# Reordering a decoder layer on one core: what stands in which half of a step, smaller pieces, and what is queued first

## The chip, the core and the metric

The kernel runs on one core of a Trainium2 chip. Its time is the time that the device takes for one execution, in microseconds; three runs are given with their median, and one more execution was profiled.

## The reference

One pre-norm decoder layer over 64 sequences of 128 tokens of width 128, with 16 heads of 8, in float32: self-attention, cross-attention to 77 context rows, and a mixture of 8 experts of which each token uses two. Cut to what matters:

```python
def _layernorm(x):                       # no weights
    return (x - mean(x)) / sqrt(var(x) + 1e-5)

def attn(x):                             # 64 x 128 x 128, heads of 8
    q, k, v = heads(x @ Wq.T / sqrt(128)), heads(x @ Wk.T), heads(x @ Wv.T)
    return (softmax(q @ k.T) @ v) @ Wff.T + bff

def xattn(x, ctx, mask):                 # ctx 64 x 77 x 128
    q, k, v = heads(x @ Wq.T + bq), heads(ctx @ Wk.T + bk), heads(ctx @ Wv.T + bv)
    s = where(mask == 0, -1e9, q @ k.T / sqrt(8))
    return (softmax(s) @ v) @ Wo.T + bo

def ffn(x):                              # 8 experts, 128 -> 512 -> 128, top 2 of a cosine gate
    g = l2norm(x @ Wp.T) @ l2norm(sim).T / temperature
    w, which = top_k(g, 2); w = softmax(w)
    return sum(w_e * (gelu(x @ W1[e] + b1[e]) @ W2[e] + b2[e]) for e in which)

x = x + attn(layernorm(x))
x = x + xattn(layernorm(x), ctx, mask)
x = x + ffn(layernorm(x))
```

## The kernel before, in words

**Groups and steps.** Four batches make a group (`GB = 4`), so there are 16 groups; each goes through a self job and a cross job, 32 jobs in all (self jobs first). `x` stays in SBUF in the tiles `xs`. The main loop of `attention` runs over steps `s`, one batch a step: in step `s` it makes the first scores of batch `a = s` (`ps`, 128x512, for the row maxima `m`), the second, transposed scores of batch `t = s - 4` (`pt`, with the maximum folded in by an extra row of `qh`), their exponentials `e`, and the product with the values (`po`) of batch `z = s - 5`. A step has two halves; each makes the scores of two of the four head groups (`score_tiles`), so a block of 16 matmuls (and in cross jobs 4 more for the mask's `bias`). There are three buffers for `ps` and two for `pt`.

**What else stands in a step.** For each job, `prologue` returns a list: normalise the group (`norm`, tile `xn`, on ScalarE), transpose it (`trans`, PE's `tp`), project the queries (`query`, `pq`), keys (`key`, `pk`) and values (`value`, `pv`). Queries and keys are copied to SBUF, written to DRAM (`d`, issued from ScalarE's queue) and read back by SP's queue with the heads spread over partitions (`qh`, `kh`, four loads each); this layout change is why each goes through DRAM. `turn` transposes the row maxima of two batches (`pm`), and sends them by way of DRAM (`md`) into a row of `qh`. `project` applies the output projection (`py`), adds it to `xs` and takes the new statistics. All these are closures in one list, `todo`; each half takes one from it after its block of scores (`next_`), and one more a step when over four wait. `turn` and `project` are put at its front. `soon` holds the division by the softmax sums and the transpose back, `late` the routing of a finished cross group (`route`), at the offsets of `LATER` in halves: normalise, transpose (`tp`), project (`pp`), pick the two largest (`largest`), `count` (with a chain on GpSimd, `ahead`), `place` (`pr`), and then scatters of the rows to their experts' places in DRAM, one a half (`sending`).

**Order on the engines.** The order of PE, VectorE (DVE) and ScalarE (ACT) is as the program is written (`manual_schedule`). GpSimd's (POOL) and SP's instructions are placed by a scheduler, which may put an instruction ahead of earlier ones when it is ready sooner; `issue_after` ties an instruction behind another in its queue.

**Experts.** The groups are in two parts, 11 and 5 groups. When all groups of a part are placed, `table` computes on VectorE which 256-row tile belongs to which expert, and where each row will lie. `experts` then goes through the tiles of a part: fetch rows (`xr`) and copy the expert's weights (`wr`), transpose (`tp`, `xT`), first layer (`ph`) with Gelu, second layer (`py`), store (`yr`). Between tiles of part 0 the rest of the attention's lists is worked off (`more`), between tiles of part 1 the results of part 0 are gathered and added (`some`); at the end those of part 1. Weights of all experts sit in SBUF (`we_s`), loaded by `load_experts`; `spare` writes blocks of zeros behind the rows.

**Start.** `clean(n)` fills the three sets of `kh`, `qh` and `vm` buffers with constants; then come the statistics of group 0, `root(0)` (a chain of eight GpSimd operations for the inverse deviation), the first prologue, the rest of the weights, statistics of groups 1 and 2.

Of the kernel before, what the change touches and what calls it, by code (L numbers as in the profile page):

```python
# [8 lines left out]
F32 = mybir.dt.float32  # L9
# [6 lines left out]
P = 128  # L16
# [9 lines left out]
LATER = (2, 3, 4, 5, 7, 8, 9, 10)  # L26
# [4 lines left out]
def decoder_layer(  # L31
# [43 lines left out]
    for g in range(1, 4):  # L75
        load_x(g)
# [32 lines left out]
    def load_experts():  # L109
        for e in range(E):  # L110
            nc.sync.dma_start(we_s[:, e, 0:F], w1[e])
            nc.sync.dma_start(
                we_s[:, e, F:WF].rearrange("p (c d) -> p c d", d=D),
                w2[e].rearrange("(c f) d -> f c d", f=P),
            )
        nc.sync.dma_start(
            we_s[:, :, WF : WF + NFC], b1.rearrange("p (e c) -> p e c", e=E)
        )
        for e in range(E):
            nc.sync.dma_start(we_s[:, e, WF + NFC :], b2[e].partition_broadcast(P))  # L120
# [44 lines left out]
    def inverse_root(r, v):  # L165

        t = work.tile([P, GB], F32, tag="newton", name="newton")[: v.shape[0], : v.shape[1]]
        nc.gpsimd.tensor_tensor(r, v, half_s[: v.shape[0], : v.shape[1]], ALU.pow)
        nc.gpsimd.tensor_tensor(t, r, r, ALU.mult)
        nc.gpsimd.tensor_tensor(t, t, v, ALU.mult)  # L170
        nc.gpsimd.tensor_scalar(t, t, -0.5, 1.5, ALU.mult, ALU.add)
        nc.gpsimd.tensor_tensor(r, r, t, ALU.mult)

    def root(g):
# [6 lines left out]
        nc.gpsimd.tensor_scalar(shift[:, at], shift[:, at], -1.0, None, ALU.mult)  # L181

    def normalised(g, tag="xn", bufs=1):
        xn = work.tile([P, GB, D], F32, tag=tag, name=tag, bufs=bufs)
        for b in range(GB):
            i = g * GB + b
            nc.scalar.activation(  # L187
                xn[:, b, :], xs[g][:, b, :], AF.Identity,
                bias=shift[:, i : i + 1], scale=rstd[:, i : i + 1],
            )  # L190
        return xn
# [74 lines left out]
    def route(g):  # L266
# [11 lines left out]
        def norm():  # L278
            v["xn"] = normalised(g, "x3", 3)
# [101 lines left out]
        def scatter(b, k, behind):  # L381
# [9 lines left out]
        return [  # L391
            norm, trans, lambda: project(0), lambda: project(1), lambda: largest(0),
# [3 lines left out]
    def table(part):  # L396

        pn = ps_m.tile([P, E], F32, tag="mm", name="pn")
        nc.tensor.matmul(pn, ones_f, part.seen, start=True, stop=True)
        M = part.rows // TILE  # L400
        N = part.tiles
        over = hp.tile([P, E, M], F32, tag="over", name="over", bufs=1)
        need = hp.tile([P, M], F32, tag="need", name="need", bufs=1)
        nc.vector.tensor_scalar(need, tid[:, :M], float(TILE), None, ALU.mult)
        count = hp.tile([P, E], F32, tag="count", name="count", bufs=1)
        nc.vector.tensor_copy(count, pn)
        nc.vector.tensor_tensor(
            over, count.unsqueeze(2).to_broadcast([P, E, M]),
            need.unsqueeze(1).to_broadcast([P, E, M]), ALU.is_gt,
        )  # L410
        nt = hp.tile([P, E], F32, tag="nt", name="nt", bufs=1)
        nc.vector.tensor_reduce(nt, over, AX.X, ALU.add)
        acc = hp.tile([P, E, E], F32, tag="acc", name="acc", bufs=1)
        nc.vector.tensor_tensor(
            acc, low, nt.unsqueeze(1).to_broadcast([P, E, E]), ALU.mult
        )
        end = hp.tile([P, E], F32, tag="end", name="end", bufs=1)
        nc.vector.tensor_reduce(end, acc, AX.X, ALU.add)
        past = hp.tile([1, N, E], F32, tag="past", name="past", bufs=1)
        nc.vector.tensor_tensor(  # L420
            past, tid[:1, :N].unsqueeze(2).to_broadcast([1, N, E]),
            end[:1].unsqueeze(1).to_broadcast([1, N, E]), ALU.is_ge,
        )
        ex = hp.tile([1, N], F32, tag="ex", name="ex", bufs=1)
        nc.vector.tensor_reduce(ex, past, AX.X, ALU.add)
        nc.vector.tensor_tensor(
            past, past, nt[:1].unsqueeze(1).to_broadcast([1, N, E]), ALU.mult
        )
        be = hp.tile([1, N], F32, tag="be", name="be", bufs=1)
        nc.vector.tensor_reduce(be, past, AX.X, ALU.add)  # L430
        nc.vector.tensor_tensor(be, tid[:1, :N], be, ALU.subtract)
        nc.vector.tensor_scalar(be, be, float(TILE), None, ALU.mult)
        rw = hp.tile([1, N], F32, tag="rw", name="rw", bufs=1)
        nc.vector.tensor_scalar(rw, ex, float(part.step), None, ALU.mult)
        nc.vector.tensor_tensor(rw, rw, be, ALU.add)
        part.row = hp.tile([1, N], I32, tag=f"prow{part.n}", name="prow", bufs=1)
        nc.vector.tensor_copy(part.row, rw)
        nc.vector.tensor_scalar(ex, ex, float(E - 1), float(WE), ALU.min, ALU.mult)
        part.wat = hp.tile([1, N], I32, tag=f"pwat{part.n}", name="pwat", bufs=1)
        nc.vector.tensor_copy(part.wat, ex)  # L440

        nc.vector.tensor_tensor(count, count, part.base, ALU.add)
        tail = hp.tile([1, E], I32, tag=f"tail{part.n}", name="tail", bufs=1)
        nc.vector.tensor_copy(tail, count[:1])
        def tail_zeros(e):
            with behind("SP"):
                r = nc.sync.value_load(
                    tail[0:1, e : e + 1], min_val=e * part.step,
                    max_val=e * part.step + part.rows,
                )  # L450
            i = nc.sync.dma_start(
                part.x[bass.ds(r, TILE), :].rearrange("(h p) d -> p h d", p=P), zero_s
            )
            last["SP"] = i.ins
            apart(i.ins, f"x{part.n}")
            part.scatters.append(i.ins)

        clearing.extend(lambda e=e: tail_zeros(e) for e in range(E))
# [5 lines left out]
        less = hp.tile([P, E], F32, tag="less", name="less", bufs=1)  # L464
        nc.vector.tensor_scalar(
            less, nt, -float(TILE), float(part.step), ALU.mult, ALU.add
        )
        sf = slot_f[:, every, :].rearrange("p b k -> p (b k)")
        off = hp.tile([P, 2 * GB * SPLIT], F32, tag="off", name="off")[:, : 2 * GB * K]
        one = hp.tile([P, 2 * GB * SPLIT], F32, tag="one", name="one")[:, : 2 * GB * K]  # L470
        nc.vector.tensor_copy(off, sf)
        for e in range(1, E):
            nc.vector.tensor_scalar(  # L473
                one, sf, float(e * part.step), less[:, e - 1 : e], ALU.is_ge, ALU.mult
            )
            nc.vector.tensor_tensor(off, off, one, ALU.subtract)  # L476
        nc.vector.tensor_copy(back[:, every, :].rearrange("p b k -> p (b k)"), off)
# [19 lines left out]
    def attention():  # L497
        jobs = [(cross, g) for cross in (False, True) for g in range(NGRP)]
        NB = len(jobs) * GB
        with (  # L500
# [27 lines left out]
            nc.vector.tensor_reduce(one, last, AX.X, ALU.add)  # L528
# [523 lines left out]
```

## Time and profile before

| | us |
|---|---|
| runs | 1321.33, 1324.6, 1330.93 (median 1324.6) |
| profiled execution | 1318.96 |
| its span, from the first to the last instruction | 1317.2 |
| PE busy | 1108.3 (84%) |
| VectorE busy | 738.7 (56%) |
| ScalarE busy | 593.8 (45%) |
| GpSimd busy | 491.8 (37%) |
| first block of scores starts | 41.33 |
| last `po` of the attention | 880.76 |
| first `ph` of the expert tiles | 899.3 |
| first `ph` of part 1 | 1104.8 |
| mean granted clock of PE | 0.919 |

Times in the profile count from the first instruction. A line of the waits names who waited for whom, the total in us, how often, and the longest. A line of a table by stretches gives the stretch and its length, then for PE, weight loads (PEld), VectorE, ScalarE and GpSimd the busy time with the number of instructions, then PE's granted clock (1.00 is full), the share of the DMA engines' time, and GB/s. A line of the timeline has start and duration, engine (a "q" behind it: the sequencer, for instance a DMA issue), source line, operation, what it writes and reads, shapes, how many follow each other, and in brackets the idle time before it and who ended it. An instruction count of PE's float32 matmuls is twice that of the program.

### The profile page before, as it was taken

The page shows a single profiled execution, that of the slowest core. Times are in us where ns is not written, and L with a number is a line of the kernel's source. Part 1 is how long each engine was busy: PE and PEld are TensorE (multiplying, and loading weights), DVE is VectorE, ACT ScalarE, POOL GpSimd, SP SyncE. Part 2 cuts the span into 40 slices and gives each one's busy share as a digit, 9 for nine tenths or more (in the row PEclk, how much of TensorE's full clock was granted, in tenths as well). Part 3 has the DMA queues.
Part 4 walks back from the last instruction along what each step waited for, and adds up shares of the span by engine and source line. Part 5 has one row for each costly group of instructions (what it writes and reads, how often), then busy time and mean ns, then how long its engine had stood idle before and what let it go on. Part 6 is the DMA issues. An engine that isn't in the chain of part 4 may idle for free. (4 is left out here: it accounts for less than half of the span.)

```text
span 1317.2 us, 39334 instructions
## 1 busy us (share of the span) xinstructions
PE 1108.3 (84%) x15925; PEld 901.9 (68%) x15925; DVE 738.7 (56%) x2129; ACT 593.8 (45%) x1374; POOL 491.8 (37%) x897
## 2 busy tenths in 40 slices
PE   2799898998999999999999997977989998666920
PEld 1577676777777777777777776756979998555910
DVE  3367676777776545666666667644454444444322
ACT  1145554555555565555655554544434443222400
POOL 5023213323121124555565554462120003777056
PEclk9589898999898999999999998997989999888965
DMA  9623121222121222232222222111223222434222
GB/s 261 147 68 75 37 54 33 56 52 55 38 66 40 51 55 55 62 71 63 67 67 65 68 65 68 34 47 57 74 75 98 73 72 83 114 108 113 59 62 78
DMA packets 120181, 94.99 MB, mean 72 GB/s; under 512 B 22712, under 2 KB 102592, under 8 KB 120000
## 3 DMA queue, kind: packets, MB, share of 16 engines
q1 hardware_dynamic: 97328, 58.73, 18.9%
q0 software_dynamic: 8192, 16.79, 4.5%
q10 hardware_dynamic: 14480, 16.96, 4.0%
q8 instruction: 125, 2.05, 0.7%
q14 instruction: 56, 0.46, 0.2%
HBM read 49.53 MB, written 42.89 MB: 70 GB/s over the span
## 5 line engine op out<-in xcount | busy, mean ns | idle before, releaser
L696 ACT ACTIVATE e<-pt 128x512 f32<-128x512 f32 (+1 forms) x512 | 276.4, 590 | 307.5 <-PE pt L659 148.9
L669 DVE TENSOR_REDUCE m<-ps 128x4 f32<-128x512 f32 (+1 forms) x512 | 274.0, 576 | 218.1 <-PE ps L659 103.1
L650 PE MATMUL ps<-kh,qh 31*128 31x128 f32 (+1 forms) x4096 | 340.7, 295 | 37.0 <-DMA kh<-d 26.0
L650 PEld LDWEIGHTS ps<-kh,qh 31*128 31x128 f32 x4096 | 284.9, 196 | 93.6 <-issue 43.4
L650 PE MATMUL pt<-qh,kh 32*128 32x128 f32 (+1 forms) x4096 | 344.2, 288 | 3.1 <-ACT e L696 1.5
L650 PEld LDWEIGHTS pt<-qh,kh 32*128 32x128 f32 (+1 forms) x4096 | 273.6, 170 | 14.7 <-ACT e L696 4.3
L883 ACT ACTIVATE hT<-ph,wr 128x256 f32<-128x256 f32 x312 | 128.9, 470 | 213.6 <-issue 186.8
L876 PE MATMUL ph<-xT,wr 128*128 128x256 f32 x624 | 163.2, 408 | 50.3 <-DVE xT L868 50.3
L382 POOL DMA_INDIRECT xr<-x,slot x128 | 129.1, 1009 | 192.0 <-ACT e L696 95.9
L929 POOL DMA_INDIRECT r<-yr,back x128 | 124.7, 974 | 191.5 <-DMA yr<-yr 152.7
L876 PEld LDWEIGHTS ph<-xT,wr 128*128 128x128 f32 x624 | 121.2, 205 | 69.6 <-DVE xT L868 54.5
L894 PEld LDWEIGHTS py<-wr,hT 128*128 128x128 f32 x1248 | 154.8, 195 | 4.6
L894 PE MATMUL py<-wr,hT 128*128 128x128 f32 x1248 | 154.4, 278 | 0.0
L711 PE MATMUL po<-e,vm 128*32 128x128 f32 (+1 forms) x4096 | 147.6, 288 | 0.0
L711 PEld LDWEIGHTS po<-e,vm 128*32 128x32 f32 (+1 forms) x4096 | 110.5, 114 | 37.2 <-issue 27.8
L177 POOL TENSOR_SCALAR var<-stat 128x4 f32<-128x4 f32 x48 | 12.0, 250 | 253.9 <-DVE stat L163 243.9
L900 DVE TENSOR_TENSOR yr<-py,wr 128x256 f32<-128x256 f32 x78 | 33.0, 423 | 119.5 <-PE py L894 119.5
L940 DVE SCALAR_TENSOR_TENSOR xs<-r,prob,xs 128x128 f32<-128x128 f32 x128 | 44.6, 351 | 92.3 <-DMA r<-yr,back 91.7
L659 PE MATMUL pt<-ident_b,bias 128*77 128x512 bf16 x256 | 93.5, 383 | 0.0
L659 PE MATMUL ps<-bias,ident_b 128*128 128x308 bf16 x256 | 76.8, 305 | 0.0
L859 DVE COPY wr<-we_s 128x1156 f32 x78 | 59.9, 769 | 26.6 <-DVE yr L900 23.0
L187 ACT ACTIVATE xn<-xs,shift,rstd 128x128 f32<-128x128 f32 x128 | 52.5, 486 | 25.0 <-POOL shift L181 16.6
(166 smaller groups left out, 1279.3 us busy)
## 6 DMA issues: line engine op xcount, KB each, us to landing
xr<-xr SPq DMA_DIRECT2D x78, 128.0 KB
yr<-yr SPq DMA_DIRECT2D x78, 128.0 KB
d<-qT ACTq DMA_DIRECT2D x32, 256.0 KB
qh<-d SPq DMA_DIRECT2D x128, 64.0 KB
xs<-in_x_dram SPq DMA_DIRECT2D x16, 256.0 KB
we_s<-in_w_dram SPq DMA_DIRECT2D x16, 256.0 KB
d<-kT ACTq DMA_DIRECT2D x16, 256.0 KB
kh<-d SPq DMA_DIRECT2D x64, 64.0 KB
```

The source lines that it names most:

```text
L187: nc.scalar.activation(xn[:, b, :], xs[g][:, b, :], AF.Identity, bias=shift[:, i : i + 1], scale=rstd[:, i : i + 1],)
L382: i = nc.gpsimd.indirect_dma_start(out=part.x, out_offset=bass.IndirectOffsetOnAxis(ap=slot[:, g * GB + b, k : k + 1], axis=0), in_=v["xn" ...
L650: nc.tensor.matmul(pt[:, r, :], v[still][rows, r, b, :], v[moving][rows, r, b, :], start="bias" not in v or r == 0, stop="bias" not in v,)
L659: nc.tensor.matmul(pt, left, right.unsqueeze(1).to_broadcast([P, HG, K]), start=False, stop=True,)
L669: nc.vector.tensor_reduce(v["m", b // 2][:, c, :, b % 2], v.pop(("ps", b, c)), AX.X, ALU.max, negate=True,)
L696: i = nc.scalar.activation(e[:K], pt[:K], AF.Exp)
L711: nc.tensor.matmul(v["o"][32 * c : 32 * c + 32, b % 2, :, j // 2, :], w[:, at : at + 32], v["e", b, c][:K, j, :].rearrange("p (n q) -> p n ...
L859: i = nc.vector.tensor_copy(v["w"], flat[:, bass.ds(w, WE)])
L876: nc.tensor.matmul(ph[:, c % 2, :], v["w"][:, c * P : (c + 1) * P], v["xT"], start=True, stop=True,)
L883: i = nc.scalar.activation(v["h"][:, n, :], ph[:, n % 2, :], AF.Gelu, bias=v["w"][:, WF + n : WF + n + 1],)
L894: nc.tensor.matmul(py[:, h, :], v["h"][:, c, h * P : (h + 1) * P], v["w"][:, F + c * D : F + (c + 1) * D], start=(c == 0), stop=(c == NFC ...
L929: inst = nc.gpsimd.indirect_dma_start(out=r, out_offset=None, in_=part.y, in_offset=bass.IndirectOffsetOnAxis(ap=back[:, i, k : k + 1], ax ...
```

## The change

- **Halves.** The second half of a step now takes from `todo`: two pieces in odd steps or when over four wait, else one. `turn` and `values` stand in the first half by themselves, after its block. `trans`, `query`, `key` and `value` of the job after next are put in `todo` at the end of a group's steps (`s % 4 == 3`).
- **Normalisation one batch a step.** `normalised` does one batch; four such closures go through a new list `bits`, two halves apart for a prologue, one a half for routing (from `NORM = 2` halves on). `xn` gets two buffers, `LATER` starts at 6.
- **Statistics.** Those of a projected pair are parted over two halves (`other`), those of the input are taken 12 steps ahead, not 9, and `x` is loaded one group earlier.
- **Tables in pieces.** `table` returns a list of 16 closures that go through `pieces`, one or two a half.
- **Start.** Statistics and `root(0)` come ahead of the clears; a clear of `vm` is tied behind a `root`; `load_rest` comes after the statistics of groups 1 and 2.
- **Loads.** An expert's weights are loaded one expert every second step from step 12 on, and the zero blocks from step 32 on, both tied behind the newest `qh` or `kh` load.
- **Passage.** The pools of the experts are opened with `reuse_waits="tile"`: a new tile waits for the earlier tiles in its own place, not for all of the earlier pool. Between tiles of part 0 one piece of any list is worked off a tile. `e` has six buffers, not eight.

The core of the diff:

```diff
-LATER = (2, 3, 4, 5, 7, 8, 9, 10)
+LATER = (6, 7, 8, 10, 11, 12, 13)
+NORM = 2
...
-    def normalised(g, tag="xn", bufs=1):
-        xn = work.tile([P, GB, D], F32, tag=tag, name=tag, bufs=bufs)
-        for b in range(GB):
...
+    def normalised(v, g, b, tag="xn", bufs=2):
+        if b == 0:
+            v["xn"] = work.tile([P, GB, D], F32, tag=tag, name=tag, bufs=bufs)
+        i = g * GB + b
+        nc.scalar.activation(
+            v["xn"][:, b, :], xs[g][:, b, :], AF.Identity,
+            bias=shift[:, i : i + 1], scale=rstd[:, i : i + 1],
+        )
...
-            def clean(n):
+            def clean(n, behind):
...
-                nc.gpsimd.memset(vms[n], 0.0)
+                with tc.issue_after(behind):
+                    nc.gpsimd.memset(vms[n], 0.0)
...
-                e = unit.tile([P, HG, P], F32, tag="e", name="e")
+                e = unit.tile([P, HG, P], F32, tag="e", name="e", bufs=6)
...
-                for b in (2 * p, 2 * p + 1):
-                    stats(g * GB + b)
-                if p == 1:
-                    root(g)
...
+                stats(g * GB + 2 * p)
+
+                def other():
+                    stats(g * GB + 2 * p + 1)
+                    if p == 0:
+                        return
                     root(g)
                     v.clear()
                     if cross:
-                        late.extend((now[0] + w, f) for w, f in zip(LATER, route(g)))
-                        if g == parts[g >= SPLIT].last - 1:
-                            late.append((0, lambda: table(parts[g >= SPLIT])))
+                        norms, steps = route(g)
+                        bits.extend((now[0] + NORM + w, f) for w, f in enumerate(norms))
+                        late.extend((now[0] + w, f) for w, f in zip(LATER, steps))
+                        part = parts[g >= SPLIT]
+                        if g == part.last - 1:
+                            late.append((now[0] + LATER[-1] + 1, lambda: pieces.extend(table(part))))
+
+                soon.append(other)
...
+            def prepare(n):
+
+                norms, steps = prologue(n)
+                bits.extend((now[0] + 2 * w, f) for w, f in enumerate(norms))
+                return steps
...
-            clean(0)
             for i in range(GB):
                 stats(i)
-            root(0)
...
+            begun = root(0).ins
+            nc.vector.tensor_reduce(one, last, AX.X, ALU.add)
+            clean(0, begun)
...
-                if s == 2 * GB:
-                    load_experts()
-                if s in range(3 * GB, 3 * GB + E - 1):
-                    for part in parts:
-                        part.spare(s - 3 * GB)
+                if s in range(3 * GB, 3 * GB + 2 * E, 2):
+                    with tc.issue_after(spread_[0].ins):
+                        load_expert((s - 3 * GB) // 2)
+                if s in range(8 * GB, 8 * GB + E - 1):
+                    with tc.issue_after(spread_[0].ins):
+                        for part in parts:
+                            part.spare(s - 8 * GB)
...
-                if s % GB == 2 and s // GB + 2 < len(jobs):
-                    todo += prologue(s // GB + 2)
+                if s % GB == 3:
+                    todo += steps
+                    steps = []
...
-                    next_()
-
-                    now[0] += 1
-                    if late and late[0][0] <= now[0]:
-                        late.pop(0)[1]()
-                    if half == 0 and z in range(NB):
-                        values(z)
+                    if half == s % 2 and n < NGRP:
+                        stats(s + 12)
+                        if b == GB - 1:
+                            root(n)
+                    if half == 0:
+                        if bits and bits[0][0] <= now[0]:
+                            bits.pop(0)[1]()
+                        if a % 2 == 0 and a in range(2, NB + 1):
+                            turn((a - 1) // GB, (a - 1) % GB // 2)
+                        if z in range(NB):
+                            values(z)
+                    else:
+                        for _ in range(2 if s % 2 or len(todo) > 4 else 1):
+                            if todo:
+                                todo.pop(0)()
+                        if bits and bits[0][0] <= now[0]:
+                            bits.pop(0)[1]()
+
+                    if late and late[0][0] <= now[0]:
+                        late.pop(0)[1]()
+                    elif pieces:
+                        pieces.pop(0)()
+                    if len(pieces) > 1 and half == 0:
+                        pieces.pop(0)()
...
-                if len(todo) > 4:
-                    next_()
-                if a < NB and a % 2:
-                    todo.insert(0, lambda n=a // GB, p=a % GB // 2: turn(n, p))
                 if z in range(NB) and z % 2:
-                    todo.insert(1, lambda n=z // GB, p=z % GB // 2: project(n, p))
+                    todo.insert(0, lambda n=z // GB, p=z % GB // 2: project(n, p))
...
-            tc.tile_pool(name="ff", bufs=3) as ff,
+            tc.tile_pool(name="ff", bufs=3, reuse_waits="tile") as ff,
...
             def more(t):
-                if rest and t % 2 == 1:
-                    rest.pop(0)()
+                rest()
```

## The prediction

> **What bounds the kernel now.** First the strip of the page: TensorE (PE) is the engine that is nearly always busy, and its granted clock is below full in several slices.
>
> ```profile
> PE   2799898998999999999999997977989998666920
> PEclk9589898999898999999999998997989999888965
> ```
>
> A matmul record lasts some 0.27 us while the next may start 0.11 us later, so a busy PE can still be waiting. So next the waits of PE, in total, over the whole run:
>
> ```profile
> PE ph L876 <- DVE xT L868: 50.3, 17, 6.1
> PE ps L650 <- DMA kh<-d: 26.0, 13, 15.7
> PE tp L201 <- ACT xn L187: 22.7, 4, 17.8
> PE pr L355 <- POOL ahead L342: 15.0, 13, 1.3
> PE pr L352 <- ACT e L332: 8.0, 1, 8.0
> ```
>
> The reader sees late loads of heads (`kh<-d`), a late normalisation (`xn`), and once a fetch of expert weights held up on VectorE (`xT`). Third, the stages (busy time of PE, PEld, DVE, ACT, POOL, then clock):
>
> ```profile
> 92.08:187.56 95.48, 88.56 (x1642) 67.69 (x1641) 67.82 (x169) 50.67 (x106) 27.93 (x71) 0.93 0.23 54
> 237.64:419.27 181.63, 170.16 (x3280) 134.27 (x3280) 135.17 (x319) 100.56 (x208) 44.24 (x120) 0.95 0.23 51
> 493.77:767.79 274.02, 260.80 (x4578) 201.53 (x4577) 169.74 (x630) 158.69 (x396) 155.38 (x285) 0.99 0.28 65
> 767.79:804.71 36.92, 27.96 (x458) 21.61 (x457) 26.99 (x100) 15.95 (x40) 17.20 (x31) 0.91 0.28 73
> 880.90:899.30 18.40, 3.69 (x24) 2.55 (x16) 10.15 (x42) 2.36 (x8) 10.88 (x25) 0.64 0.22 65
> ```
>
> A group is 4 batches, so 4 steps of 2 halves. These are 4 self groups (23.9 us each), 8 self groups (22.7), 10 cross groups (27.4), one cross group that also holds the table of part 0 (36.9), and the passage to the expert tiles. Last, inside a self group, the timeline:
>
> ```profile
> 357.41 0.66 PE L201 MATMUL tp<-ident,xn 128*128 128x128 f32 x4
> 357.55 1.08 ACT L696 ACTIVATE e<-pt 128x512 f32<-128x512 f32 x2 [2.86 <-PE pt L650]
> 358.20 0.37 PE L650 MATMUL pt<-qh,kh 32*128 32x128 f32 x1
> 358.69 0.37 PE L650 MATMUL pt<-qh,kh 32*128 32x128 f32 x1
> 359.77 1.13 PE L594 MATMUL pq<-xnT,wq_s 128*128 128x512 f32 x2
> 360.83 1.08 PE L711 MATMUL po<-e,vm 128*32 128x128 f32 x32
> ```
>
> The block of scores that starts at 358.00 needs the two `pt` buffers, which the exponentials of the block before free at 358.15 and 358.64. Only `tp` (0.59 us) stood between, so the block took 1.77 us (to 359.77). The next one, behind `pq` and `po`, started at 361.84 and took 1.10 us. So each block wants about 1 us of other PE work behind it.
>
> **The change, part by part.**
>
> *Balance of halves.* From PE's start-to-start times an unhindered self group is 8 blocks x 1.10 + 4 `po` x 1.01 + 2 `pm` x 0.21 + `tp` 0.59 + `pq` 1.06 + `pk` 0.96 + `pv` 0.98 + 2 `py` x 0.64 = 18.1 us. Before, `pm`, `pq` and `po` share a half while `tp` or `py` stands alone: three blocks of a group are 0.65 us late. In the changed kernel's instruction order every first half holds `po` (1.01) and every second one `pq`, `py`+`pk`, `pv` or `py`+`tp` (0.98 to 1.60): these stalls go. VectorE needs 17.5 us a group (its busy time in one), 97% of 18.1; as it works in order I take 18.9 (between 18.1 and 20.5).
>
> *Late loads.* One load's chain in a self group:
>
> ```profile
> 367.71 1.12 PE L606 MATMUL pk<-xnT,wk_s 128*128 128x512 f32 x2
> 369.49 0.34 ACTq L582 DMA_DIRECT2D d<-kT  x1
> 371.56 1.30 SPq L585 DMA_DIRECT2D kh<-d  x4
> 374.69 0.37 PE L650 MATMUL ps<-kh,qh 31*128 31x128 f32 x1 [0.87 <-DMA kh<-d]
> ```
>
> From the end of `pk` (368.67) to the first quarter of `kh` is 6.0 us, to the second 7.0. In steps 8 to 27 of the changed order `pk` stands two and a half steps ahead of its first block (over 10 us): no wait. At step 26 the two pieces of gate weights enter the same list; it takes 6 pieces a group, which is just what a group puts in, so from step 28 on everything stands one step later: `tp`, `py`+`pq`, `pk`, `py`+`pv`. Then 1.10 + 1.01 + 1.10 + 0.64 + 0.98 = 4.8 us lie behind `pk`: PE waits 1.15, the second tile some 0.85 more. After such a wait (1.00 us before 419.27) the granted clock is 0.50 from 421.93 to 425.35, 3.41 us, worth 1.7 us of work; it follows somewhat more than half of them: 1.0. With VectorE eased by the pause, 18.1 + 0.3 + 2.0 + 1.0 = 21.4. In cross groups the same place has 6.2 us behind `pk`, and the chain is 5.3 (pk 595.48, ends 596.0; load landed about 601.3): no wait.
>
> "TensorE: Matmul & The Clock Gate" of the Trainium skill (section on HAM oscillation) says that the clock falls after idle gaps of about 3.4 us, and elsewhere that a busy window of that length restores it. The rows above show half clock after 1.0 us of idling, and 47.8 us at 0.50 (29.40 to 77.19) though PE was busy 27.8 of the 28.7 us from 41.33 to 70.02. By the page the nine late loads would cost 9 us less and the first steps some 13 us less; the trace decides, and the sum has neither.
>
> *Normalisation a batch a step, `x` statistics 3 steps earlier, `LATER`.* The four `xn` pieces (0.4 us each) come two halves apart behind the exponentials; ScalarE has 12.6 us of work in a group. The 1.6 us waits of `tp` for `xn` in steps 12 to 24 go (in the 18.9). `place` now has a block, `tp` and `po` between itself and `count`: of the 1.32 us wait for `ahead` I keep 0.3 (0 to 1.3).
>
> *Cross groups.* Of 27.37 us, 1.2 are late blocks and 1.32 the wait of `pr`: 24.85. Back come 0.4 for the half with `pk` alone (0.52 us), 0.25 for blocks behind `py`, `pq` and `pp`, and the 0.3: 25.8 (25.0 to 26.8). Groups without routing (steps 64 to 75) 22.7.
>
> *Table in pieces.* PE stood 7.1 us at 793 behind VectorE's burst for part 0 (group 36.9 against 27.4) and 6.1 us at 972 for part 1, with 6.8 us of half clock each. Pieces of 0.4 to 0.9 us fit into VectorE's idle 10 us of a cross group, and behind tiles of 3.73 us with 1.6 us of VectorE work. If that cover failed, the 9.5 us come back.
>
> *Start.* SP's queue before ran 17 weight loads, 8 bias rows and 5 zero blocks ahead of the first `qh`, issued at 29.57; first block 41.33. After: 16 loads of `x` (4.2 MB, at the 261 GB/s of the first slice 16 us), then context and mask. The second mask load waits for GpSimd's `bias`, which stands behind `root(1)` and the clear: statistics of group 0 from 4.3 us, xn 11.3, statistics of group 1 at 16.1, root 19.2, clear 21.2, bias 22.5; `qh` issues at 23, eight loads, first block at 29 (26 to 34): -12.3. The weights go behind loads in steps 12 to 26: up to 2 us each in front of a `qh<-md` that has 1.2 us of slack; I add 3 us. Steps 0 to 7: 50.7 becomes 48.
>
> *Passage and tiles.* `pr` waited 8.0 us there for routing that hung on GpSimd's scatters; that piece now comes several tiles later, and the new pools wait for tiles, not for pools. Left are the last `aT` and `py`, three `wr` copies x 0.77, reading the index (1.2), `xT`: 9 us instead of 18.4 (7 to 14). Tiles of part 0: 51 x 3.73 + 9 = 199 instead of 205.5 (two more table loads of ScalarE, 1.3 us each, are taken as hidden by its 1.7 us of slack a tile). From part 1 on (212 us) nothing changes: its tiles wait for gathers that the change leaves alone.
>
> *Sum*, against the profiled execution (1318.96 us, span 1317.2): start -12.3; steps 0 to 7 -2.7; steps 8 to 27: 124.3 to 5 x 18.9 + 8 (gate weights stall as before) + 3 = 105.5, -18.8; steps 28 to 63: 202.9 to 9 x 21.4 = 192.6, -10.3; 64 to 75: 74.5 to 68, -6.5; 76 to 119: 310.9 to 11 x 25.8 = 283.8, -27.1; 120 to the last `po` 0; passage -9; tiles -6.5. Together -93, so 1226. The median of the runs shown is 5.6 us above that execution: 1231. A measurement here can tell about 1% from no change.
>
> **The rivals.** (1) The head loads come in time in steps 28 to 63 too, since a late group pushes itself back: 9 x 2.5 less, 1209. For it: the wait is 1 us of 6; against: the list has no slack to catch up. (2) VectorE sets the pace of all self groups, at 22.5: 5 x 3.6 + 9 x 1.1 = 28 more, 1259. For: 97% load; against: three buffers of `ps`, and halves that differ by no more than 0.7 us. (3) The change doesn't do what it says: blocks stay late for another reason, and only start, passage and tables gain (-40): 1285. Against: buffer release and block start agree within 0.05 us. (4) Slower: a `turn`'s `qh<-md` (pm, copy, out, SP's queue, back) becomes the wait of every second step, since shorter steps leave it 8 us. Its longest in the trace is 10.3 (pm 93.78, `pt` released 104.1), a usual one 6.4 (365.29; load issued 369.60, plus 2.1 as `d<-kT`). Two self steps would be L + 1.3, two cross steps L + 2. With the 40 us of (3) in hand it decides from L = 11.7; at 12.5 self groups are 27.6 (+4.2 x 14), cross 29 (+1.6 x 15): 1366. Against: SP's order puts it behind at most four head loads.
>
> **How the numbers follow.** Forecast 0.66 (its own range 1214 to 1250), rival (1) 0.14, (2) 0.10, (3) 0.04, (4) 0.06. The range, 1200 to 1266, takes in (1) and (2) with the bounds of cross groups. Faster by over 1%: 0.92; within 1%: 0.02, from the upper end of (3); slower: 0.06.
>
> **What would show it.** Right: blocks of 1.1 us behind `tp`; first block near 29; `kh<-d` waits only in steps 28 to 63; cross groups near 25.8; no 7 us stop near a table; first `ph` 9 us behind the last `po`. Wrong: `ps` waiting for `DVE m` or `pt` for `qh<-md` many times, or self groups above 22.

## The result, and the profile after

The changed kernel takes 1411.34 us (median of four runs, 1404.9 to 1415.25) against 1323.4 us before: a ratio of 1.065 (95% interval 1.059 to 1.071). It is 6.5% slower, where 1231 us and "faster" were forecast. The profiled execution took 1415.25 us, with a span of 1413.5. Its strip of the page:

```profile
PE   2899879889898888888888888999899999766930
PEclk8599989989899878899999989995899999898975
```

PE is no longer at 9 over the middle of the span but at 8, and its clock drops again and again: the loss is spread over the whole attention, not at one spot. The waits (total, how often, longest):

```profile
PE ps L674 <- DMA kh<-d: 114.4, 31, 13.9
PE ph L941 <- DVE xT L933: 41.1, 15, 4.0
PE tp L200 <- ACT xn L187: 12.5, 1, 12.5
PE pt L674 <- DMA qh<-md: 10.5, 4, 3.8
...
PE pr L354 <- POOL ahead L341: 1.2, 3, 0.6
...
SPq L575 <- POOL bias L596: 53.1, 11, 6.4
```

The waits that the change was to remove are gone: `tp` waits for `xn` only at the very start, `pr` for `ahead` hardly at all, `ph` 9 us less. But the waits for `kh` went from 26.0 to 114.4 us, 88 us more, with half clock behind many of them; that outweighs all that was gained. The last line is SP's: its queue stood 53 us, 11 times, in front of a mask load that waited for GpSimd. That wait is not new; in the kernel before SP stood almost as long for the same `bias`:

```profile
SPq L554 <- POOL bias L572: 50.5, 15, 4.4
```

So what counts is what stands behind the mask load in the queue. The table by stretches, for the same pieces of work as before:

```profile
83.51:173.90 90.39, 83.28 (x1641) 66.27 (x1640) 69.22 (x169) 51.28 (x105) 25.28 (x68) 0.94 0.44 86
231.82:433.69 201.87, 176.93 (x3281) 138.66 (x3281) 135.30 (x312) 101.55 (x208) 44.40 (x116) 0.91 0.25 55
520.58:863.98 343.40, 281.75 (x4578) 213.29 (x4577) 181.46 (x606) 165.33 (x399) 150.03 (x274) 0.88 0.20 51
863.98:898.75 34.77, 27.36 (x459) 20.71 (x458) 19.14 (x64) 16.90 (x41) 16.86 (x30) 0.90 0.21 55
984.70:998.70 14.00, 6.75 (x33) 4.86 (x24) 10.56 (x44) 3.93 (x12) 9.41 (x15) 0.62 0.17 52
```

A cross group takes 34.3 us (third line, ten groups), not 27.4; the group that held the table's burst is now no longer than the others (fourth line), so the table in pieces did what it was meant to. By stage, in us, with the prediction's terms and with one kernel of the experiments (the changed kernel with two pieces of a list moved, below):

| stage | before | predicted | after | two pieces moved |
|---|---|---|---|---|
| to the first block | 41.3 | 29 | 33.2 | 33.5 |
| steps 0 to 7 | 50.8 | 48 | 50.3 | 44.3 |
| steps 8 to 27 | 124.3 | 105.5 | 124.6 | 126.3 |
| steps 28 to 63 | 202.9 | 192.6 | 225.6 | 187.1 |
| steps 64 to 75 | 74.5 | 68 | 86.9 | 65.4 |
| steps 76 to 119 | 310.9 | 283.8 | 378.2 | 287.1 |
| 120 to the last `po` | 76.0 | 76.0 | 86.0 | 81.8 |
| passage | 18.6 | 9 | 14.0 | 14.0 |
| tiles of part 0 | 205.5 | 199 | 199.1 | 198.4 |
| rest | 212.4 | 212 | 215.7 | 210.7 |

Now one cross group in the timeline of the changed kernel, with the queue of SP, GpSimd and PE in order of time:

```profile
686.85 0.27 SPq L609 DMA_DIRECT2D kh<-d  x1
687.40 0.20 POOL L172 TENSOR_TENSOR rnorm<-rnorm,newton 128x4 f32<-128x4 f32 x1
...
689.25 1.28 POOL L193 TENSOR_TENSOR xs<-xs,bo_s 128x512 f32<-128x512 f32 x1
689.91 0.33 PE L674 MATMUL ps<-kh,qh 31*128 31x77 f32 x1
...
691.76 1.27 POOL L596 TENSOR_SCALAR bias<-mask 128x308 bf16<-128x308 int32 x1
693.05 0.40 SPq L575 DMA_DIRECT2D mask<-in_mask_dram  x1
693.50 0.50 SPq L573 DMA_DIRECT2D ctx<-in_ctxT_dram  x1
694.04 1.02 SPq L609 DMA_DIRECT2D kh<-d  x3
697.22 0.46 PE L674 MATMUL ps<-kh,qh 31*128 31x77 f32 x1 [6.87 <-DMA kh<-d]
```

The scheduler put a mask load between the first and the other three `kh` loads. It waits for GpSimd's `bias` (to 693.03), which reads the one buffer of the tile `mask`. The three `kh` loads, whose data had been ready since before 686.85, go out behind it, 7 us late. PE finds the first quarter at 689.91, stands 6.87 us for the second, and then runs at half clock (0.50 from 694.1 to 700.9). In nine of the eleven groups of steps 76 to 119 this wait is 6.4 to 7.0 us. In the kernel before the four `kh` loads stood together and the mask load behind them:

```profile
598.91 1.30 SPq L585 DMA_DIRECT2D kh<-d  x4
600.25 0.36 SPq L552 DMA_DIRECT2D ctx<-in_ctxT_dram  x1
604.90 0.40 SPq L554 DMA_DIRECT2D mask<-in_mask_dram  x1
```

In the self groups of steps 28 to 63 the waits for `kh` come where they were expected, but are 1.5 to 3.3 us long (eight of them), not 1.15:

```profile
298.27 1.32 SPq L609 DMA_DIRECT2D qh<-d  x4
300.95 0.34 ACTq L606 DMA_DIRECT2D d<-kT  x1
301.40 0.51 SPq L709 DMA_DIRECT2D qh<-md  x1
305.34 1.30 SPq L609 DMA_DIRECT2D kh<-d  x4
...
308.42 0.58 PE L674 MATMUL ps<-kh,qh 31*128 31x128 f32 x1 [2.87 <-DMA kh<-d]
```

`d<-kT` now goes out while the four `qh` loads, issued 1.7 to 2.7 us before it, are still landing; `kh` follows it by 4.4 us, where it was 2.07 before, with `d<-kT` going out 4.8 us after the last `qh` load. The eight groups of steps 32 to 63 agree: 0.1 to 1.7 us after the last `qh` load and 3.2 to 4.6 us to the issue of `kh`; in the kernel before 2.9 to 4.8 us after it and 2.0 to 2.7 us. "DMA: Bandwidth & Descriptors" of the Trainium skill (section "Issuing engines are not separate DMA queues") says that transfers issued by different engines run on the same 16 DMA engines and interleave; the 4.4 against 2.07 us agree with it.

### The profile page after: what moved, and what is told of

Its sections match the earlier page's. It is cut to its first block, busy times and chain, and to the rows that moved or that the text cites. A ratio compares the mean times of both kernels' runs of the same rounds, so it can differ in the third digit from the quotient of the medians.

```text
span 1413.5 us, 39417 instructions
## 1 busy us (share of the span) xinstructions
PE 1153.0 (82%) x15925; PEld 931.3 (66%) x15925; DVE 755.6 (53%) x2129; ACT 605.4 (43%) x1376; POOL 502.6 (36%) x897
## 4 chain that ended last, share of the span: by engine, by line
PE 60%; DMA 18%; POOL 7%; issue 6%; DVE 4%; ACT 2%; SPq 2%; ACTq 0%; DVEq 0%; POOLq 0%
PE ps L674 12%; PE ph L941 9%; PE py L959 8%; PE po L735 8%; PE pt L674 7%; DMA r<-yr,back 7%; DMA kh<-d 5%; DMA d<-kT 4%; PE pt L683 3%; PE ps L683 3%; PE pq L618 2%; PE tp L200 2%; DMA qh<-md 1%; PE py L774 1%; PE pk L630 1%
## 5 line engine op out<-in xcount | busy, mean ns | idle before, releaser
L674 PE MATMUL ps<-kh,qh 31*128 31x128 f32 (+1 forms) x4096 | 358.3, 306 | 121.3 <-DMA kh<-d 114.4
L674 PEld LDWEIGHTS ps<-kh,qh 31*128 31x128 f32 x4096 | 301.5, 207 | 197.2 <-issue 132.5
L674 PE MATMUL pt<-qh,kh 32*128 32x128 f32 (+1 forms) x4096 | 365.5, 304 | 11.7 <-DMA qh<-md 10.5
L674 PEld LDWEIGHTS pt<-qh,kh 32*128 32x128 f32 (+1 forms) x4096 | 294.4, 182 | 20.6 <-issue 11.7
L941 PE MATMUL ph<-xT,wr 128*128 128x256 f32 x624 | 164.9, 412 | 41.3 <-DVE xT L933 41.1
L959 PEld LDWEIGHTS py<-wr,hT 128*128 128x128 f32 x1248 | 157.9, 199 | 4.7
L735 PE MATMUL po<-e,vm 128*32 128x128 f32 (+1 forms) x4096 | 156.8, 300 | 0.0
L735 PEld LDWEIGHTS po<-e,vm 128*32 128x32 f32 (+1 forms) x4096 | 116.8, 120 | 37.2 <-issue 29.0
L683 PE MATMUL pt<-ident_b,bias 128*77 128x512 bf16 x256 | 104.0, 423 | 0.0
L683 PE MATMUL ps<-bias,ident_b 128*128 128x308 bf16 x256 | 81.7, 324 | 0.0
L187 ACT ACTIVATE xn<-xs,shift,rstd 128x128 f32<-128x128 f32 x128 | 62.5, 493 | 40.8 <-DMA bk_s<-in_bk_dram 8.4
```

The lines of the kernel that those rows point to most:

```text
L187: nc.scalar.activation(v["xn"][:, b, :], xs[g][:, b, :], AF.Identity, bias=shift[:, i : i + 1], scale=rstd[:, i : i + 1],)
L674: nc.tensor.matmul(pt[:, r, :], v[still][rows, r, b, :], v[moving][rows, r, b, :], start="bias" not in v or r == 0, stop="bias" not in v,)
L683: nc.tensor.matmul(pt, left, right.unsqueeze(1).to_broadcast([P, HG, K]), start=False, stop=True,)
L735: nc.tensor.matmul(v["o"][32 * c : 32 * c + 32, b % 2, :, j // 2, :], w[:, at : at + 32], v["e", b, c][:K, j, :].rearrange("p (n q) -> p n ...
L941: nc.tensor.matmul(ph[:, c % 2, :], v["w"][:, c * P : (c + 1) * P], v["xT"], start=True, stop=True,)
L959: nc.tensor.matmul(py[:, h, :], v["h"][:, c, h * P : (h + 1) * P], v["w"][:, F + c * D : F + (c + 1) * D], start=(c == 0), stop=(c == NFC ...
```

## The experiments

Three theories for the waits for `kh`: A, the mask load in SP's queue; B, VectorE or GpSimd sets the pace of a cross group; C, the same for self groups. The kernels are numbered e1 to e12. The first eight ran once each, beside the kernel before at 1326.46 (e1 to e4) and 1328.21 us (e5 to e8), also one execution each; e9 ran once, e10 to e12 four times. The three sets of four ran on three different chips. All are the changed kernel with an edit, but for the one that says otherwise.

**Two mask buffers (e1).**

```diff
-                m = grp.tile([P, GB, S2], I32, tag="mask", name="mask", bufs=1)
+                m = grp.tile([P, GB, S2], I32, tag="mask", name="mask", bufs=2)
```

> The changed kernel with two buffers for the tile `mask` instead of one, so that its load no longer waits for GpSimd's `bias` of the job before. Theory A (in a cross group three of the four `kh` loads stand in SP's queue behind a mask load that waits for GpSimd): the 6.4 to 7.0 us waits of `ps` for `kh` shrink to 1 to 3.5 us, what is left because the context load between the `kh` loads waits for `pv`, which stands right ahead of the block; cross groups fall from 33.4-34.7 us to 28-30, the whole to 1345-1375. Theory B (VectorE's or GpSimd's work on a cross group sets its length, and the wait for `kh` is only where it shows): cross groups stay above 32, the whole within 12 us of 1411. Self groups keep their 25 us under both.

Measured: 1319.81 us, 91 us less than the changed kernel. Its ten cross groups (table by stretches) and SP's queue in one of them:

```profile
519.03:790.46 271.43, 262.02 (x4577) 200.23 (x4576) 178.94 (x606) 163.94 (x400) 150.40 (x274) 0.98 0.25 64
```

```profile
657.40 0.36 SPq L573 DMA_DIRECT2D ctx<-in_ctxT_dram  x1
657.81 0.66 SPq L609 DMA_DIRECT2D kh<-d  x2
660.45 0.40 SPq L575 DMA_DIRECT2D mask<-in_mask_dram  x1
```

27.1 us a group, 25.8 to 26.6 in eight of the ten (32.7 and 28.1 in the others): the excess is gone, and B falls. But not as A had it: the mask load, by count that of one group further on, still goes out 0.03 us after a `bias` ends (660.42 on GpSimd). SP stands 16.9 us for `bias` in all. What counts is the order that the scheduler now chose, with the mask load behind the `kh` loads. A's remainder of 1 to 3.5 us didn't come either: of the `kh` loads only the two for the second half of the step stand behind the context load, and they land in time. Self groups stay as they were (202.1 us for steps 32 to 63).

**`bias` traced earlier (e2).** With one mask buffer, `bias` is computed in `norm(0)` of a job, not in `norm(3)`:

```diff
                     normalised(v, g, b)
+                    if b == 0 and cross:
+                        v["bias"] = ...          # and the tensor_scalar that fills it
                     if b < GB - 1:
                         return
```

> The changed kernel with one mask buffer as it is, but with GpSimd's `bias` traced after the first of the four normalised batches instead of after the last; `add_row` stays behind the last. Theory A: the mask load finds its buffer free some 10 us earlier, so the waits of `ps` for `kh` in cross groups fall as with two buffers, groups 28-30 us, the whole 1345-1375. Theory B: within 12 us of 1411. If the time falls with two buffers and not here, it was not the lateness of `bias` but the buffer's queue position.

Measured: 1418.05 us; ten cross groups take 343.5 us, as without the edit. The edit doesn't do what it says: in both kernels `bias` runs 1.9 us after the start of a group's first step, since the scheduler has put it at the same place of GpSimd's order. SP's order stays too, with the mask load ahead of three `kh` loads. That the change traces `bias` later ("one batch a step") is thus not what makes it late; between A and B this run decides nothing.

**The loads tied behind `kh` (e5).** One mask buffer, `bias` as it was:

```diff
                 def norm(b):
-                    if b == 0:
-                        loads(n + 1)
                     normalised(v, g, b)
                     if b < GB - 1:
                         return
+                    loads(n + 1)                 # its two DMAs: issue_after(spread_[0].ins)
```

> The changed kernel, one mask buffer, list as it is; only the context and mask loads of the next job are traced after the last of the four normalised batches and tied behind the newest `kh` load, so that SP's queue holds all four `kh` loads ahead of them. Theory A, put sharper (it is the place in SP's queue alone; neither the buffer nor GpSimd's `bias` need be any earlier): cross groups 26 to 27.5 us as with two mask buffers, the whole 1305-1330. If the single buffer itself is what costs: cross groups above 31, the whole above 1370. Self groups stay at 25 us under both.

Measured: 1306.27 us; cross groups of steps 76 to 115:

```profile
509.85:774.42 264.57, 257.39 (x4578) 196.83 (x4577) 178.95 (x606) 163.73 (x399) 150.32 (x274) 1.00 0.27 66
```

26.5 us a group, with the same buffers and `bias` where it was: it is the order in SP's queue alone. No mask or context load runs ahead of the first `qh` now either, so the first block starts at 30.2 instead of 33.2.

**Four buffers for `bias` (e9).**

```diff
-                        v["bias"] = grp.tile([P, GB, S2], BF16, tag="bias", name="bias", bufs=3)
+                        v["bias"] = grp.tile([P, GB, S2], BF16, tag="bias", name="bias", bufs=4)
```

> The changed kernel with four buffers for `bias` instead of three, one mask buffer, everything else as it is. Theory A2 (why tracing `bias` earlier did nothing: its own buffer is the one that the last `pt` block of the group before still reads, so GpSimd cannot write it, the mask load cannot go, and `kh` cannot go, until one half before `kh` is needed): a fourth buffer lets `bias` and the mask load run a group ahead, cross groups 26 to 27 us, the whole 1310-1332. Rival (it is GpSimd's work ahead of `bias`, the two chains of inverse roots, scatters and `add_row`, that makes it late): cross groups stay above 32, the whole above 1395.

Measured: 1368.42 us, beside the kernel before at 1371.73 (median of seven), 3.3 to 3.4% more than beside e1 to e8; so this one and the last three are read as ratios. 0.998 is where two mask buffers were (0.995), not where the changed kernel is (1.065). The waits of about 7 us in cross groups are gone. The trace:

```profile
659.22 0.61 SPq L609 DMA_DIRECT2D kh<-d  x2
662.67 0.36 SPq L573 DMA_DIRECT2D ctx<-in_ctxT_dram  x1
663.07 0.66 SPq L609 DMA_DIRECT2D kh<-d  x2
664.44 1.27 POOL L596 TENSOR_SCALAR bias<-mask 128x308 bf16<-128x308 int32 x1
665.74 0.40 SPq L575 DMA_DIRECT2D mask<-in_mask_dram  x1
```

By count `bias` and the mask load do run a group ahead, as A2 had it: the `bias` at 664.44 is the eleventh of 16, in the changed kernel the one at this place in the steps (691.76) is the tenth. But it still comes 1.9 us after the start of the first step (662.57), and the mask load right behind it; with one buffer more and one group ahead it needs the buffer of the same earlier group. So an earlier `bias` is not what helps: the `kh` loads now stand ahead of the mask load. The 27.4 to 30.2 us a group lie above what was expected; on this chip the cross groups of e10 to e12 were longer too (last section).

**The gate weights out of the list (e3).** From step 26 on two extra pieces kept the list `todo` one place behind. Here they go into `late`:

```diff
-                    todo.append(finish_weights)
-                    todo.append(gate_weights)
+                    late.append((0, finish_weights))
+                    late.append((0, gate_weights))
```

> The changed kernel with the two pieces of gate weights in the list `late` instead of `todo`, so that `tp`, `pq`, `pk` and `pv` stay one half step earlier in the order from step 28 on; one mask buffer. Theory A: self groups of steps 28 to 63 lose their 1.5 to 3.3 us waits for `kh` and the half clock after them, 25.1 us to 20-21.5, some -37 us over nine groups, -8 in steps 64 to 75. In cross groups the four `kh` loads now stand ahead of the mask load, but a `qh<-md` stands behind it: groups 26 to 30 us. The whole 1270-1330. Theory C (the self groups are bound by VectorE or by `qh<-md` and wait for `kh` only because it is there): self groups above 23.5.

Measured: 1250.2 us, less than A expected. Its waits and its table for steps 32 to 63 and 76 to 115:

```profile
PE pt L674 <- DMA qh<-md: 18.1, 9, 4.2
PE ps L674 <- DMA kh<-d: 14.3, 1, 14.3
```

```profile
225.11:391.15 166.04, 159.66 (x3282) 127.17 (x3281) 134.20 (x315) 102.53 (x209) 45.90 (x120) 0.99 0.29 66
456.57:717.33 260.76, 253.86 (x4578) 194.22 (x4577) 179.40 (x607) 166.87 (x400) 149.91 (x274) 1.00 0.26 67
```

Only the one wait at the start is left of 31. Self groups take 20.8 us (20.18 where nothing is late), so C falls; cross groups 26.1. With `pk` one place earlier, all four `kh` loads are issued ahead of the mask load (654.85 to 659.58 against 667.98 in one group), and one move of two closures cures both losses. SP waits for `bias` even longer in this kernel:

```profile
SPq L575 <- POOL bias L596: 80.8, 13, 7.4
```

That is 80.8 us against 53.1, and costs nothing, as nothing urgent stands behind the mask load: PE waits for no `qh<-md` in steps 76 to 119.

**Both edits (e4).**

> Both edits: two mask buffers, and the gate weights out of `todo`. Theory A: the two causes add up: self groups of steps 28 to 63 at 20-21.5 us, cross groups at 25-27 us, as the prediction had them; the whole 1265-1300. Theories B and C: self groups above 23.5 or cross groups above 32; the whole above 1350.

Measured: 1262.02 us: self groups 18.8 to 24.5, cross groups 26.1, as with the list's edit alone; the second cure adds nothing. The 12 us more lie in steps 0 to 7 (52.4 against 44.3 us) and steps 36 to 55; see the last section for the first.

**The same edit in the kernel before (e6).**

> The kernel before, with one edit: the two pieces of gate weights go into `late` instead of `todo`. It is the control for two terms of the prediction. If the late `kh` loads of the kernel before have the same cause as those of the changed one (the list stands behind by the two pieces), its 26 us of waits for `kh` mostly go and its self groups of steps 28 to 63 fall from 22.5 to 21.5-22, cross groups from 27.4 to 26.2-27, the whole 1290-1312. If the balance of halves is worth what the prediction said, self groups then still lie 1 to 3 us above the 20.2-20.9 us of the changed kernel with the same edit; if it is worth nothing, they come to the same 20.2-21.

Measured: 1346.96 us, 19 us slower than the kernel before (one execution each): my expectation failed. Its waits, and six self groups (steps 32 to 55):

```profile
PE tp L201 <- ACT xn L187: 44.0, 23, 17.8
PE ps L650 <- DMA kh<-d: 17.7, 2, 17.1
```

```profile
246.38:389.77 143.39, 132.68 (x2461) 100.90 (x2460) 101.11 (x251) 76.20 (x158) 36.69 (x102) 0.93 0.22 49
```

The waits for `kh` go, as expected, but `tp` now waits 1.6 us in every self group (0.7 in a cross group) for `xn`, which is normalised in one lump just before, and in each of the six groups half clock for 3.41 us begins 0.9 us after this wait. In the kernel before the late list hid that. Of the 19 us, 16 lie in steps 76 to 119 (327.0 against 310.9 us). The run makes a control: with the list in the same place a self group takes 23.9 us with the old order and 20.2 (unhindered) with the new one. Of these 3.7 us, 1.6 are the `xn` wait and up to 1.7 the half clock behind it; both go with normalisation a batch a step. For all else that the change moves in such a group, the halves among it, some 0.4 us are left.

**Expert weights behind `qh<-md` (e7).** In steps 12 to 27 PE waited for `qh<-md`. With the list's edit, one such place in SP's queue, and PE:

```profile
112.69 1.29 SPq L609 DMA_DIRECT2D kh<-d  x4
114.03 0.36 SPq L111 DMA_DIRECT2D we_s<-in_w_dram  x1
114.44 0.43 SPq L112 DMA_DIRECT2D we_s<-in_w_dram  x1
114.91 0.50 SPq L120 DMA_DIRECT2D we_s<-in_b_dram  x1
115.45 0.52 SPq L709 DMA_DIRECT2D qh<-md  x1
...
121.25 0.55 PE L674 MATMUL pt<-qh,kh 32*128 32x128 f32 x1 [2.50 <-DMA qh<-md]
```

```diff
-                if s in range(3 * GB, 3 * GB + 2 * E, 2):
-                    with tc.issue_after(spread_[0].ins):
+                if s in range(3 * GB + 1, 3 * GB + 1 + 2 * E, 2):
+                    with tc.issue_after(spread_[1].ins):      # the newest qh<-md
```

> The changed kernel with the gate weights in `late`, and with the loads of the expert weights tied behind a `qh<-md` load in odd steps instead of behind the newest `qh` or `kh` load in even ones. Theory D (the waits of `pt` for `qh<-md` in steps 16 to 27, 2.5 to 4.2 us each, are the weights' bytes standing ahead of it in the DMA queues: 5.7 us from issue to landing instead of 2.0): these waits go, steps 8 to 27 fall from 126 to 108-115 us, the whole from 1250 to 1230-1240. Rival E (such a wait comes from the chain itself, as in rival 4 of the prediction, and the weights are only near it): steps 8 to 27 above 121, the whole above 1244.

Measured: 1246.06 us; steps 8 to 27 fall from 126.3 to 115.4 us, and PE's waits for `qh<-md` in them from 10.1 to 4.6. D holds for most of it (groups at 16 and 20: 21.1 and 20.7 us, from 24.8 and 25.3); waits of 1.49 and 3.07 are left in this stage. In steps 28 to 63 both kernels have some 7 us more of such waits, most of them where no expert weights are loaded, so E has a share too. The total fell by less, as steps 0 to 7 took 5 us longer in this execution.

**The gate weights' piece cut in two (e8).**

> As the kernel with the moved expert weights, and the gate weights' piece cut in two: the transpose `pt` comes eight halves after GpSimd's chain that it needs. PE's wait for `bvb` of 4.9 us in step 26 goes, with some half clock after it: 5 to 8 us less than the kernel with the moved expert weights, 1223-1234.

Measured: 1252.68 us, not less. The wait of 4.9 us for `bvb` is gone (0.9 us for VectorE is left in its place), and steps 24 to 31 fell from 53.2 to 47.8, but steps 0 to 7 took 4 us more and the drain after step 124 some 7 more, with half clock from 799.3 to 836.8. With one execution each this doesn't tell the two apart.

**Putting it together.** Tied loads and the list's edit (e10); with the moved expert weights (e11); with the cut piece too (e12).

> Context and mask loads tied behind `kh`, and the gate weights in `late`: the two cures by another way than two mask buffers. If the causes are the place in SP's queue and the place in the list, and nothing else, the time is that of the gate weights' edit alone less the 2 to 4 us at the start (no context or mask load ahead of the first `qh`): 1242-1252. If the single edit of the list had already cured all of it by luck of the scheduler's order, nothing changes: 1247-1254.

> The same with the expert weights tied behind `qh<-md` in odd steps. Theory D: another 8 to 14 us less in steps 8 to 27, 1230-1243; rival E: no difference to the kernel without it.

> The same with the gate weights' piece also cut in two (PE no longer waits 4.9 us for GpSimd's `bvb`): another 4 to 6 us less, 1225-1238. If the half clock that follows a stall, not the stall, sets the difference, up to 8 us less; if the wait only moves, none.

Measured, against 1371.73 us of the kernel before on the same chip: 1322.23 (ratio 0.963, 0.957 to 0.969), 1316.96 (0.961, 0.955 to 0.967) and 1301.04 us (0.950, 0.942 to 0.957). All three beat the kernel before, and so, by these ratios, the changed one (1.065). The last gained more than I gave the cut piece; the difference between the first two lies within the scatter. As ratios the expectations (0.94 down to 0.92) were missed by 2 to 3%. Steps 8 to 27 did what was expected of them (126.1, 119.2, 115.8 us); cross groups, 28.8 to 30.7 us from step 84 on, did not.

## Why the prediction was wrong

- **The step that failed** is the sentence on cross groups: 6.2 us of work behind `pk` against a chain of 5.3, "no wait". The 5.3 was read from the trace of before, where nothing stood between `d<-kT` and `kh` in SP's queue. The change reorders that queue too: the mask load went in between the first `kh` load and the other three, and it hangs on another engine. PE waited 6.4 to 7.0 us in nine groups, with half clock behind it, where the sentence had nothing. At the start I had followed this very load ("The second mask load waits for GpSimd's `bias`") and not asked where its successors stand. That is 283.8 predicted against 378.2, 94 us. Four kernels (two mask buffers, four of `bias`, tied loads, an earlier `pk`) take it away, and all four by the order of this queue: SP still stands for `bias` in each (16.9, 18.7, 23.6 and 80.8 us).
- **Late loads in self groups** were put in the right place for the right reason (the two gate pieces), but mis-sized: 1.15 us became 1.5 to 3.3, because I took `d<-kT` at the 2.07 us that it needed without `qh`'s loads, which now run beside it (4.4 us). That these loads are the cause is read from the groups of two kernels; no edit tests it. With half clock behind it: 25.1 us a group instead of 21.4; 33 us over steps 28 to 63, and 19 in 64 to 75, which I had priced with no wait.
- **Steps 8 to 27**: 105.5 predicted, 124.6 measured. Expert weights ahead of `qh<-md` had 3 us in all; its landing took 4.5 to 5.8 us instead of 2.0 in three groups, and PE waited 10.0 us there. An unhindered group takes 20.2 us, not 18.9, 2.1 us more than the sum of 18.1 with its eight blocks of 1.10: three of the four blocks behind `po` take 1.34 to 1.38, and the two behind `tp` and `pq` 1.4 us more together (1.60 and 1.98 in the group from 225.11 to 245.29 us of the kernel with the moved pieces). The exponentials that free their `pt` buffers come late on ScalarE. Ahead of the block behind `pq` (230.10) they stand behind an `xn` piece that waits for GpSimd, and behind `mt`; ahead of the one at 233.09 behind the next `xn` piece:

```profile
228.82 0.49 ACT L187 ACTIVATE xn<-xs,shift,rstd 128x128 f32<-128x128 f32 x1 [1.07 <-POOL shift L181]
229.86 1.08 ACT L720 ACTIVATE e<-pt 128x512 f32<-128x512 f32 x2 [0.40 <-ACT mt L706]
231.86 0.49 ACT L187 ACTIVATE xn<-xs,shift,rstd 128x128 f32<-128x128 f32 x1 [0.42 <-ACT qT L623]
232.26 1.06 ACT L720 ACTIVATE e<-pt 128x512 f32<-128x512 f32 x2
```

  I had looked to VectorE for the remainder. This is read from one group, and no run tests it.
- **Halves**: three blocks 0.65 us late were to go, 1.95 us a group. By the control some 0.4 us of gain is left for them; the late blocks of the point above took their place.
- **Right**: the two pieces of the list; `xn` a batch a step (1.6 us a group by the control, up to 3.3 with the half clock); the wait for `ahead` (0.6 us at most); the tables; tiles of part 0 (199.1 against 199). With the two pieces moved, steps 28 to 119 take 539.6 us against 544.4 in my sum. That is luck in part: the sum had late loads in it and an unhindered group too short.
- **Start**: `qh` was to issue at 23 and does at 22.99; but its four loads go out over 6.1 us, with waits of SP that the profile puts down to `qh` itself and to the small load `bq_s`, so the first block is at 33.2 instead of 29. **Passage**: 14.0 instead of 9; `pr`, `py` and the first `ph` still wait 1.55, 1.56 and 3.6 us one after another.
- **The rivals**: the slower one had the wrong transfer. In the changed kernel `qh<-md` is late only in the steps with expert weights, 10.5 us in all; with the two pieces moved there are five more waits of 1.2 to 2.0 us in steps 28 to 59, so its chain has little to spare. (By its own terms the rival's 1366 is 1367.) Rival (2) was wrong on VectorE: with 17.2 us of work in a group of 20.2 no block of the self groups of steps 8 to 63 waited for it. That a load waiting for another engine holds up the queue behind it was in none of them.

## What to carry to other kernels

Where a scheduler places the DMA issues, look at the new order of that queue before you price a chain that goes through it: one load that waits for another engine costs nothing behind the urgent loads and its whole wait ahead of them, at every turn, and a scheduler may flip the two for any small reason. Take the duration of a transfer from a place where the same other transfers are in flight. And a wait that goes may have been cover for another: the same two moved closures saved 161 us in one kernel and cost 19 in the other.

## What was not expected of the hardware

- Steps 0 to 7 differ by 9 us between executions with the same order there. The granted clock is 0.50 from 21 to 24 us on in each and is full for the rest of these steps from 48.7 us in the kernel with the moved pieces (44.3 us for these steps), from 69.5 in the changed kernel (50.3) and from 75.6 in the one with the cut piece (53.5). Stretches at half clock there last 27.31, 17.07 and 51.20 us, multiples of 3.413 us; "TensorE: Matmul & The Clock Gate" of the Trainium skill (Part 1, the HAM clock gate) has a free-running window of 3413 ns, which agrees.
- In e9 to e12 the cross groups with routing took 2 to 4 us more than in the kernels before them (30.7 in e10 against 26.3 with the list's edit and 26.4 with tied loads), and self groups no more. PE stood inside blocks for some 0.3 us at a time with nothing to wait for on record, in e10 and e11 with 3.4 us at half clock behind it in most of these groups; the kernel before was 44 to 45 us slower there too. These four ran on a chip of their own; whether that is the cause stays open.
